# A count of TensorE's work that decides when products are issued and when their readers are written down, in a one-core Mamba and mixture-of-experts kernel

## The chip, the cores and the metric

The kernel runs on one core of a Trainium2 chip. The core has a matrix engine (TensorE, PE in the profile, with its weight loads as PEld), a vector engine (VectorE, DVE), an engine for activations and copies (ScalarE, ACT), GpSimd (POOL), which here multiplies and issues indirect DMAs, and SyncE (SP), which issues nearly all other DMAs. Each engine takes its instructions in the order in which the program wrote them. Matrix products land in PSUM, which has eight banks of 128 x 512 floats here. The metric is the time of one execution on the device in microseconds (us).

## The reference

A sequence of 4096 rows of width 256 goes through a Mamba block and a mixture of experts, each with a residual and a layer norm. Cut to what matters:

```python
# x: (1, 4096, 256) float32
xc, z = split(x @ W_in.T)                        # 512 + 512
u = silu(causal_conv(xc, taps of 4) + b_conv)
dt = softplus(u @ W_dt.T + b_dt);  Bm, Cm = u @ W_B.T, u @ W_C.T
# scan over time, 512 channels x 16 states
h = exp(dt * A) * h + dt * u * Bm;  y = sum_n(h * Cm)
x = layernorm(x + (y * silu(z)) @ W_out.T)

shared = (silu(x @ sg.T) * (x @ su.T)) @ sd.T
w = softmax(x @ router.T);  top = top_k(w + bias, 6);  w = w[top] / sum(w[top])
out = sum over the 6 experts of w_e * (silu(gate_e(x)) * up_e(x)) @ down_e + shared
x = layernorm(x + out)
```

There are 32 experts with 128 inner features; the shared expert has 256.

## The kernel before

**Tiling.** The 4096 rows go in NC = 8 chunks of 512. The scan is a chain of 512 units, 64 for each chunk: one unit is one state of 16 for one group of 128 channels over 512 steps of time. In a unit the scan (L1312) and the product with C (L1319) run on DVE, the exp (L1177) and the copy of the last state (`keep`, L1204) on ACT, dt*u*B (`du`, L1166) on POOL, and four transposes that add into y (L1223, `summed`, three units behind) on PE. The rows of B and C are broadcast to 128 partitions by DMA (`load_bc`, tiles bb and cb), three to four pairs of units ahead. There are six buffers of du, six of hc and three of h.

**Side work.** Everything else is written between the units by Python generators ("threads"). After each unit's instructions `step()` gives every living thread one turn, in the order in which they were appended; a thread writes a few instructions and yields. So a `yield` is a distance in the engines' program order, not a wait on the chip. `rounds(k)` is k yields; `beside(gens, gap)` starts generators `gap` turns apart and gives each a turn. The threads:

- `front(c+1)` (L889), during chunk c: loads and transposes x, projects it (px, L919), the convolution by taps as products (pv, L942), the gate of chunk c (`gate`, pz, L1039), silu (L961), B and C (pb, L969), then `stepped` (pd, L985, four products for the step sizes, with four ACT operations and two of DVE each), and the log part (L1015 to L1021). It ends with `load_x` four rounds later.
- `tail(c-1)` (L1068), during chunk c: reads the scan's result (pgt, L1080), the output projection (px, L1097), the layer norm, then `prepare` (L293): transposes, the router (pr, L323), top 6, `ranked` (pk, L438, and the places of each row in a sorted store xs), and after it the shared expert (`shared`: spg, spu, L370 and L384; spo, L402), whose result goes to acc by DMA.
- `copies(c)` (L563): 24 indirect DMAs on POOL that put the chunk's rows into xs, at most one a round, with a rest after every third.
- `load_rows(c)`: waits until the copies of chunk c-1 are written, then loads the rows for the tail.
- `tiles` (L733) and `pair` (L701): tiles of 128 sorted rows, two at a time. `loaded` issues the DMAs of the rows (xt), of the weights (gu, dn) on SP; `pair` transposes (pt, L668), multiplies (pg, L709), tanh and products (L717 to L721), the down projection (po, L727), and scatters into acc on POOL (L691). After a pair is begun, `tiles` rests four rounds. The tiles of a chunk are to be had once its copies are written, two chunks after its scan began.
- `walls`, `cleared`, `blanked`: DMAs alone. After the scan `through_all` (L1345) does the last two chunks' tiles with all weights held in SBUF, then `finish` does the last layer norm.

At the sixth unit before a chunk's end the front is drained: `drain` calls `step()` without writing units until the front has ended. `multiply` asserts at unit 33 of a chunk that the gate's silu is written.

**PSUM.** While the scan runs, side work has three banks. `room()` yields while all are held; `bank()` takes the next by rotation, whichever is free; `free()` counts down. A reader is written one or two rounds after its product:

```python
        def room():                       # L140
            while held[0] >= len(pools):
                yield
        def bank(name):                   # L144
            held[0] += 1
            turn[0] += 1
            return pools[turn[0] % len(pools)].tile([P, T], F32, tag="mm", name=name)
```

Of the kernel before, what the change touches and what calls it, by code (L numbers as in the profile page):

```python
# [60 lines left out]
def kernel(  # L61
# [70 lines left out]
    ps_m = ctx.enter_context(tc.tile_pool(name="ps_m", bufs=BANKS, space=PSUM))  # L132
# [3 lines left out]
    held, turn = [0], [0]  # L136

    pools = [ps_m] * BANKS

    def room():  # L140
        while held[0] >= len(pools):
            yield

    def bank(name):  # L144
        held[0] += 1
        turn[0] += 1
        return pools[turn[0] % len(pools)].tile([P, T], F32, tag="mm", name=name)

    def free():
        held[0] -= 1  # L150

# [11 lines left out]
    threads = []  # L163

    apart_from = [False]

    def step():
        threads[:] = [g for g in threads if alive(g)]
# [124 lines left out]
    def prepare(c):  # L293
# [9 lines left out]
        def turned(k):  # L303
            yield from room()
            pt = bank(f"pt_{c}_{k}")
            for b in range(nb):
                nc.tensor.transpose(pt[:, ts(b, P)], row[:, b, ts(k, P)], ident)
            yield
            nc.scalar.copy(x1T[:, k, :Tc], pt[:, :Tc])
            free()  # L310

        yield from beside([turned(k) for k in range(KD)], 1)
        nc.scalar.copy(
            row[:, :nb, ID : ID + 1],
            rows_f[:, AT[c] // P : AT[c] // P + nb].unsqueeze(2),
        )
        yield
        yield from room()
        pr = bank(f"pr_{c}")
        lg = pr[:, : nb * E].rearrange("p (b e) -> p b e", e=E)  # L320
        for b in range(nb):
            for k in range(KD):
                nc.tensor.matmul(  # L323
                    lg[:, b, :], x1T[:, k, ts(b, P)], rw[:, k, :],
                    start=(k == 0), stop=(k == KD - 1),
                )
        yield
        yield
        mx = stat.tile([P, NB], F32, tag="mx", name=f"mx_{c}")[:, :nb]
        nc.vector.tensor_reduce(mx, lg, AX.X, ALU.max)  # L330
        nc.vector.tensor_sub(prob, lg, mx.unsqueeze(2).to_broadcast([P, nb, E]))
        free()
        yield
        nc.scalar.activation(prob, prob, AF.Exp)
        yield
        sm = stat.tile([P, NB], F32, tag="sm", name=f"sm_{c}")[:, :nb]
        nc.vector.tensor_reduce(sm, prob, AX.X, ALU.add)
        nc.vector.reciprocal(sm, sm)
        nc.vector.tensor_mul(prob, prob, sm.unsqueeze(2).to_broadcast([P, nb, E]))


        score = stat.tile([P, NB, E + 2], F32, tag="score", name=f"score_{c}")[:, :nb]
        left = stat.tile([P, NB, E + 2], F32, tag="left", name=f"left_{c}")[:, :nb]
        top = stat.tile([P, NB, 8], F32, tag="top", name=f"top_{c}")[:, :nb]
        nc.vector.memset(score[:, :, E:], PAD)
        nc.vector.tensor_add(
            score[:, :, :E], prob, sbias.unsqueeze(1).to_broadcast([P, nb, E])
        )
        for b in range(nb):
            nc.vector.max(top[:, b, :], score[:, b, :E])  # L350
        nc.vector.memset(top[:, :, TOP_K:], PAD)
        yield
        for b in range(nb):
            nc.vector.match_replace(left[:, b, :], top[:, b, :], score[:, b, :], GONE)
        nc.vector.tensor_tensor(mask, left[:, :, :E], score[:, :, :E], ALU.not_equal)
        nc.vector.tensor_mul(prob, mask, prob)
        sm = stat.tile([P, NB], F32, tag="psm", name=f"psm_{c}")[:, :nb]
        nc.vector.tensor_reduce(sm, prob, AX.X, ALU.add)
        nc.vector.tensor_scalar(sm, sm, NORM_MIN, 2.0, ALU.max, ALU.mult)
        nc.vector.reciprocal(sm, sm)  # L360
        nc.vector.tensor_mul(
            row[:, :nb, WT:RW], prob, sm.unsqueeze(2).to_broadcast([P, nb, E])
        )
        yield from ranked(c, mask)

        def shared(i):
            yield from room()
            pg = bank(f"spg_{c}_{i}")
            for k in range(KD):
                nc.tensor.matmul(  # L370
                    pg[:, :Tc], sg_w[:, k, ts(i, P)], x1T[:, k, :Tc],
                    start=(k == 0), stop=(k == KD - 1),
                )
            yield
# [5 lines left out]
            free()  # L380
            yield from room()
            pu = bank(f"spu_{c}_{i}")
            for k in range(KD):
                nc.tensor.matmul(  # L384
                    pu[:, :Tc], su_w[:, k, ts(i, P)], x1T[:, k, :Tc],
                    start=(k == 0), stop=(k == KD - 1),
                )
            yield
            yield
            nc.vector.tensor_mul(hm, hm, pu[:, :Tc])  # L390
            free()
            hms.append(hm)

        for i in range(NSH):
            yield from shared(i)
        for h in range(nb // 2):
            yield
            yield from room()
            po = bank(f"spo_{c}_{h}").rearrange("p (b d) -> p b d", d=D)
            for b in range(2):  # L400
                for i in range(NSH):
                    nc.tensor.matmul(  # L402
                        po[:, b, :], hms[i][:, ts(2 * h + b, P)], sd_w[:, i, :],
                        start=(i == 0), stop=(i == NSH - 1),
                    )
            yield
            yield
            base = q1.tile([P, T], F32, tag="sg", name=f"base_{c}_{h}")
            base = base.rearrange("p (b d) -> p b d", d=D)
            nc.vector.tensor_add(base, po, row[:, 2 * h : 2 * h + 2, :D])  # L410
            free()
            yield from rounds(3)
            lo = AT[c] + 2 * h * P
            i = nc.sync.dma_start(
                acc[0][lo : lo + 2 * P, :].rearrange("(b p) d -> p b d", p=P), base
            )
            for j in adds:
                tc.declare_no_dep(i.ins, j, reason="rows of earlier chunks")

    def ranked(c, mask):  # L420
# [13 lines left out]
        yield from room()  # L434
        pk = bank(f"pk_{c}")
        flat = pk[:, : nb * E]
# [8 lines left out]
        yield  # L445
# [34 lines left out]
        free()  # L480
# [180 lines left out]
    def turned_rows(j, xt):  # L661
        yield from take("xsT", 2)
        yield from room()
        pt = bank(f"pt_{j}")
        pt4 = pt.rearrange("p (i k t) -> p i k t", i=2, k=KD)
# [3 lines left out]
        yield  # L669
        xT = q2.tile([P, 2, KD, P], F32, tag="xsT", name=f"xsT_{j}")  # L670
        nc.scalar.copy(xT.rearrange("p i k t -> p (i k t)"), pt)  # L671
        free()
# [6 lines left out]
    def added(j, po, wt, no, behind):  # L679
# [6 lines left out]
        free()  # L686
# [14 lines left out]
    def pair(j, xt, wt, gu, dn):  # L701

        xT, no = yield from turned_rows(j, xt)
        yield from room()
        pg = bank(f"pg_{j}").rearrange("p (h i t) -> p h i t", h=2, i=2)
        for h in range(2):
# [6 lines left out]
        give("xsT")  # L713
        yield from take("hm", 2)
        yield
# [6 lines left out]
        free()  # L722
        yield
        yield from room()
        po = bank(f"po_{j}").rearrange("p (i d) -> p i d", i=2)
        for i in range(2):
# [3 lines left out]
        yield  # L730
        yield from added(j, po, wt, no, False)

    def tiles(items):  # L733
# [4 lines left out]
        def begin(upto):  # L738
            while begun[0] < upto:
# [5 lines left out]
                yield from rounds(4 if items[k][2] else 3)  # L745
# [732 lines left out]
```

## Time and profile before

| what | value |
|---|---|
| median of three runs (range) | 1814.09 us (1813.79 to 1816.94) |
| the profiled execution | 1827.13 us, its span 1825.4 us |
| first scan starts, last ends | 61.1 us, 1559.5 us |
| chunks 0 to 7 of the scan | 145.7, 171.9, 184.9, 202.5, 205.1, 197.8, 195.5, 195.0 us |
| from the last scan to the first scatter of `through_all` | 39.5 us |
| mean granted clock of PE | 0.83 |

The chunks are read from the starts of every 64th scan in DVE's timeline. The first chunk has no tail and no pairs beside it, the second no pairs, the third eight pairs, chunks 3 to 7 some ten to twelve each; the last has no front. A position within a chunk ("unit 48") counts the scans written ahead of an instruction on DVE. Counted in this way the first chunk-wide steps of the tail stand at units 11 and 17 (L1105), the router's first reader at 26 (L330), the places at 32 or 33 (L484), the shared expert's readers at 43 to 59 (L379 to L410), the four pd readers at 29 to 39 (L997), and the last row of the log part at 46 to 48 (L1020).

In the lines of a profile, `idle before` is time in which the engine stood still ahead of that instruction, with what ended it. A wait's line has the total in us, how often, and the longest.

### The profile page before, as it was taken

How to read it: one execution, taken by the hardware profiler on the slowest of the kernel's cores; microseconds unless marked ns; L12 is line 12 of the kernel's file. 1: busy time of each engine (PE TensorE's matmuls, PEld its weight loads, DVE VectorE, ACT ScalarE, POOL GpSimd, SP SyncE). 2: the span in 40 equal slices, each digit the busy share in tenths (PEclk: the TensorE clock that was granted, in tenths of full speed). 3: DMA queues.
4: the chain of work that ended last, by engine and by line, in shares of the span. 5: the costliest groups of instructions: out<-in, count | busy, mean ns of one | idle time of the engine just before them, and what ended most of it. 6: DMA issues, size and time to landing. Idle time of an engine off the chain costs nothing. (4 is left out here: it accounts for less than half of the span.)

```text
span 1825.4 us, 23592 instructions
## 1 busy us (share of the span) xinstructions
PE 1310.7 (72%) x6068; PEld 916.8 (50%) x6068; DVE 1399.5 (77%) x2341; ACT 961.9 (53%) x2057; POOL 1184.6 (65%) x941
## 2 busy tenths in 40 slices
PE   7386696779675967699577977698677664885940
PEld 3243453456453634565465645565465543764730
DVE  4789979997998679868997789868998886441216
ACT  4567564547563656447554656457654532432533
POOL 0555544766587547776579548965797668466864
PEclk8597697679896988899788987899789787897975
DMA  9543782688577957797698858996699989975978
GB/s 254 152 119 105 231 290 78 161 228 239 134 177 204 251 146 171 213 248 193 127 246 216 242 133 193 248 245 176 151 249 274 274 192 264 231 120 112 145 105 344
DMA packets 307246, 359.62 MB, mean 197 GB/s; under 512 B 62368, under 2 KB 230048, under 8 KB 307104
## 3 DMA queue, kind: packets, MB, share of 16 engines
q1 hardware_dynamic: 266400, 302.82, 59.3%
q0 software_dynamic: 38592, 55.17, 16.9%
q8 instruction: 51, 0.84, 0.2%
q14 instruction: 91, 0.75, 0.1%
q10 hardware_dynamic: 2112, 0.05, 0.1%
HBM read 251.77 MB, written 106.15 MB: 196 GB/s over the span
## 5 line engine op out<-in xcount | busy, mean ns | idle before, releaser
L1166 POOL TENSOR_TENSOR du<-wall,bb 128x512 f32<-128x512 f32 x512 | 703.5, 1425 | 396.8 <-DVE h L1312 203.5
L1312 DVE TENSOR_TENSOR_SCAN h<-h,hlast,du 128x512 f32<-128x512 f32 x512 | 657.2, 1284 | 71.4 <-POOL du L1166 27.2
L1223 PE MATMUL y<-ident,hc 128*128 128x128 f32 x2048 | 340.2, 309 | 120.7 <-DVE hc L1319 105.4
L1177 ACT ACTIVATE h<-wall,aneg 128x512 f32<-128x512 f32 x512 | 354.0, 692 | 121.8 <-DVE hc L1319 96.6
L1319 DVE TENSOR_TENSOR hc<-h,cb 128x512 f32<-128x512 f32 x512 | 354.1, 692 | 55.4 <-DMA cb<-bcd 13.7
L1223 PEld LDWEIGHTS y<-ident,hc 128*128 128x128 f32 x2048 | 278.2, 161 | 217.6 <-DVE hc L1319 131.5
L691 POOL DMA_INDIRECT acc<-yt,no x136 | 215.5, 1584 | 93.2 <-ACT yt L685 44.8
L578 POOL DMA_INDIRECT xs<-row,at x192 | 191.7, 998 | 75.3 <-issue 33.7
L1204 ACT COPY hlast<-h 128x1 f32<-128x1 f32 x448 | 70.9, 158 | 252.2 <-DVE hc L1319 239.7
L727 PE MATMUL po<-dn,hm 128*128 128x256 f32 x272 | 96.5, 489 | 117.3 <-issue 58.1
L709 PE MATMUL pg<-xsT,gu 128*128 128x128 f32 x1088 | 147.6, 293 | 29.2 <-ACT xsT L671 25.4
L709 PEld LDWEIGHTS pg<-xsT,gu 128*128 128x128 f32 x1088 | 140.3, 206 | 46.3 <-ACT xsT L671 29.7
L691 POOL DMA_INDIRECT acc<-ytl,no x68 | 105.9, 1558 | 39.9 <-issue 20.1
L727 PEld LDWEIGHTS po<-dn,hm 128*128 128x128 f32 x272 | 60.1, 240 | 142.4 <-issue 68.5
L985 PE MATMUL pd<-wall 128*128 128x512 f32 x256 | 123.7, 631 | 10.2 <-ACT yt L685 5.9
L942 PE MATMUL pv<-wall 128*128 128x512 f32 x224 | 106.5, 619 | 7.4 <-ACT wall L924 3.8
L1362 DVE SCALAR_TENSOR_TENSOR gt<-gt,pg 128x256 f32<-128x256 f32 x34 | 14.3, 420 | 110.8 <-ACT gt L1360 68.3
L668 PE MATMUL pt<-ident,xt 128*128 128x128 f32 x408 | 71.9, 305 | 36.5 <-DMA xt<-xs 17.2
L668 PEld LDWEIGHTS pt<-ident,xt 128*128 128x128 f32 x408 | 56.8, 159 | 56.3 <-DMA xt<-xs 19.2
L985 PEld LDWEIGHTS pd<-wall 128*128 128x128 f32 x256 | 49.8, 204 | 65.0 <-issue 57.0
L720 DVE SCALAR_TENSOR_TENSOR gt<-gt,pg 128x256 f32<-128x256 f32 x68 | 28.1, 414 | 63.5 <-ACT gt L717 46.9
L671 ACT COPY xsT<-pt 128x512 f32<-128x512 f32 x102 | 59.5, 583 | 30.8 <-PE pt L668 22.7
(196 smaller groups left out, 1891.0 us busy)
## 6 DMA issues: line engine op xcount, KB each, us to landing
bb<-bcd SPq DMA_DIRECT2D x256, 256.0 KB
cb<-bcd SPq DMA_DIRECT2D x256, 256.0 KB
gu<-in_gate_up_t_dram SPq DMA_DIRECT2D x136, 256.0 KB
xs<-blank SPq DMA_DIRECT2D x55, 578.0 KB
xt<-xs SPq DMA_DIRECT2D x204, 128.5 KB
dn<-in_down_t_dram SPq DMA_DIRECT2D x136, 128.0 KB
wall<-acc SPq DMA_DIRECT2D x24, 512.0 KB
acc<-blank SPq DMA_DIRECT2D x16, 512.0 KB
```

The lines of the kernel that those rows point to most:

```text
L578: i = nc.gpsimd.indirect_dma_start(out=xs, out_offset=bass.IndirectOffsetOnAxis(ap=at[:, b, k : k + 1], axis=0), in_=row[:, b, :], in_offs ...
L668: nc.tensor.transpose(pt4[:, i, k, :], xt[:, i, ts(k, P)], ident)
L691: a = nc.gpsimd.indirect_dma_start(out=acc[(j + i) % LANES], out_offset=bass.IndirectOffsetOnAxis(ap=no[:, i : i + 1], axis=0), in_=yt[:, ...
L709: nc.tensor.matmul(pg[:, h, i, :], gu[i][:, k, ts(h, P)], xT[:, i, k, :], start=(k == 0), stop=(k == KD - 1),)
L727: nc.tensor.matmul(po[:, i, :], hm[:, i, :], dn[i], start=True, stop=True)
L942: nc.tensor.matmul(pv, taps[:, m, k, :], xin[:, m, k : k + Tc], start=(k == 0), stop=(k == TAPS - 1),)
L985: nc.tensor.matmul(pd, w_dt[:, k, ts(m, P)], u[:, k, :], start=(k == 0), stop=(k == M - 1),)
L1166: nc.gpsimd.tensor_mul(parts(q, du), u, row_for(q, 0))
L1177: nc.scalar.activation(h[:, ts(i, Tc)], dt_of[c][:, m + i, :], AF.Exp, scale=aneg[:, m + i, n : n + 1],)
L1223: nc.tensor.matmul(y_of[c, g][b // 2][:, b % 2, ts(m + j - 2 * g, P)], hc[:, ts(j * nb + b, P)], ident, start=(opens and j == 0 and b % 2 ...
L1312: nc.vector.tensor_tensor_scan(h, h, du_of.pop(q), hlast[:, n, m : m + 1], ALU.mult, ALU.add)
L1319: nc.vector.tensor_mul(parts(q, hc), parts(q, h), row_for(q, 1))
```

## The change

There are five parts.

1. A count of TensorE's work. `room(work)` gets a price for the product to be issued. `out_at` adds up the prices, `done_at` follows by PACE = 2.5 a round. While more than LITTLE = 2.3 is outstanding and the new product would bring it over 2.5, the thread yields. This holds while `paced` is set, from the first unit to the last.
2. Readers. `made()` takes the place of the yield between a product and its reader: one yield, and then more until the count has that product done. After the scan it is one yield.
3. Banks. A bank is taken from a list of free ones and goes back to it when its reader is written, each bank a pool of its own.
4. Order. `step()` sorts the threads: tail, tiles, pairs, front, others. The front's gap goes from 3 to 2. A pair may load once fewer than three have their gu products outstanding, and `tiles` rests one round after a pair of its own, not four.
5. In chunks but the last, routing and shared expert run beside each other, the second starting two rounds after the first.

```diff
+    PACE, LITTLE = 2.5, 2.3
+    out_at, done_at, paced = [0.0], [0.0], [False]
+
+    def room(work):
+        def full_up():
+            left = out_at[0] - done_at[0]
+            return held[0] >= len(pools) or (
+                paced[0] and left > LITTLE and left + work > PACE
+            )
+
+        while full_up():
+            yield
+        out_at[0] += work
+
+    def made(at=None):
+
+        at = out_at[0] if at is None else at
+        yield
+        while paced[0] and done_at[0] < at - 0.01:
             yield
 
     def bank(name):
         held[0] += 1
-        turn[0] += 1
-        return pools[turn[0] % len(pools)].tile([P, T], F32, tag="mm", name=name)
-
-    def free():
+        newest[0] = spare.pop(0)
+        return pools[newest[0]].tile([P, T], F32, tag=f"mm{newest[0]}", name=name)
+
+    def free(which):
         held[0] -= 1
+        spare.append(which)
...
+    FIRST = {"tail": 0, "tiles": 1, "pair": 2, "front": 3}
...
     def step():
+        done_at[0] = min(out_at[0], done_at[0] + PACE)
+
+        threads.sort(key=lambda g: FIRST.get(g.__name__, len(FIRST)))
         threads[:] = [g for g in threads if alive(g)]
...
+        if c < NC - 1:
+            yield from beside([routing(), sharing()], 2)
+        else:
+            yield from routing()
+            yield from sharing()
...
     def pair(j, xt, wt, gu, dn):
 
         xT, no = yield from turned_rows(j, xt)
-        yield from room()
+        yield from room(1.9)
         pg = bank(f"pg_{j}").rearrange("p (h i t) -> p h i t", h=2, i=2)
+        mine = newest[0]
...
         give("xsT")
+        give("gu")
+        at = out_at[0]
         yield from take("hm", 2)
-        yield
+        yield from made(at)
...
-                yield from rounds(4 if items[k][2] else 3)
+                yield from rounds(1 if items[k][2] else 3)
...
             if weights is not None:
+                yield from take("gu", 3)
                 yield from take("dn", 4)
...
-                yield from rounds(3 if c < NC - 1 else 2)
+                yield from made()
+                yield
                 part = row_of[c][:, 2 * h : 2 * h + 2, :D]
...
+        done_at[0], paced[0] = out_at[0], True
...
-                    mains.append(front(c + 1, 3))
+                    mains.append(front(c + 1, 2))
...
         scanned.append(True)
+        paced[0] = False
```

The other places go the same way: `room(w)`, the bank's number kept, `made()` for a yield, `free(mine)`. The prices:

| product | price | in a chunk |
|---|---|---|
| front: transposes of x, px, pv, pz, pb, pd | 0.8, 1.9, 3.6, 1.9, 3.6, 3.6 | 2, 4, 4, 4, 1, 4 |
| tail: pgt, px of L1097, transposes, pr, pk | 0.65, 3.6, 0.8, 1.4, 1.6 | 4, 2, 2, 1, 1 |
| tail: spg, spu, spo | 1.9, 1.9, 1.9 | 2, 2, 2 |
| pair: pt, pg, po | 0.65, 1.9, 1.0 | 12 each |

## The prediction

> **What bounds the kernel now.** I read the page's lines first, then the windows view of the scan, then the waits of VectorE (DVE), then windows inside a chunk.
>
> ```profile
> span 1825.4 us, 23592 instructions
> PE 1310.7 (72%) x6068; PEld 916.8 (50%) x6068; DVE 1399.5 (77%) x2341; ACT 961.9 (53%) x2057; POOL 1184.6 (65%) x941
> ...
> L1312 DVE TENSOR_TENSOR_SCAN h<-h,hlast,du 128x512 f32<-128x512 f32 x512 | 657.2, 1284 | 71.4 <-POOL du L1166 27.2
> ...
> L1319 DVE TENSOR_TENSOR hc<-h,cb 128x512 f32<-128x512 f32 x512 | 354.1, 692 | 55.4 <-DMA cb<-bcd 13.7
> ```
>
> Each of the 512 units costs DVE 1.284 + 0.692 us. The first scan starts at 61.1 us, the last ends at 1559.5; the next window is that whole stretch. Columns are length, then busy time (and instructions) of PE, PEld, DVE, ACT, POOL, then granted clock, DMA share, GB/s.
>
> ```profile
> 61.10:1559.50 1498.40, 1114.38 (x5170) 772.09 (x5170) 1288.12 (x2005) 823.96 (x1738) 1011.41 (x807) 0.83 0.76 200
> ```
>
> DVE is busy 1288 of 1498 us, so 210 us are idle and 86% is work that this change leaves as it is. The waits of DVE in that stretch:
>
> ```profile
> DVE gt L720 <- ACT gt L717: 43.3, 10, 7.1
> DVE h L1312 <- POOL du L1166: 27.2, 23, 2.3
> DVE h L1312 <- ACT h L1177: 26.4, 18, 3.5
> DVE h L1312 <- ACT hlast L1204: 16.2, 8, 3.9
> DVE hc L1319 <- DMA cb<-bcd: 13.7, 6, 3.9
> ```
>
> 43 + 26 + 16 us end at ScalarE (ACT), and ACT's own timeline tells why. At 1024.3 us it had waited 5.44 us for the convolution's product, with the tanh and the scan's exp queued behind:
>
> ```profile
> 1018.19 0.69 ACT L1177 ACTIVATE h<-wall,aneg 128x512 f32<-128x512 f32 x1
> 1024.32 0.69 ACT L947 ACTIVATE wall<-pv,bcv 128x512 f32<-128x512 f32 x1 [5.44 <-PE pv L942]
> 1026.10 0.38 ACT L717 ACTIVATE gt<-pg 128x256 f32<-128x256 f32 x1 [1.10 <-PE pg L709]
> ```
>
> So a reader written one round after its product stops ACT, then DVE, then GpSimd (POOL). Is TensorE (PE) then the bound? Units 6 to 25 of chunks 3, 4, 5 and 6, in windows:
>
> ```profile
> 576.50:639.00 62.50, 57.27 (x273) 39.78 (x273) 43.12 (x58) 34.91 (x79) 35.30 (x28) 0.95 0.89 245
> 787.00:844.50 57.50, 55.70 (x260) 37.13 (x258) 44.73 (x57) 34.22 (x75) 38.52 (x30) 0.96 0.91 246
> 986.50:1048.60 62.10, 60.41 (x279) 40.61 (x280) 43.74 (x59) 36.74 (x80) 41.16 (x31) 0.92 0.92 241
> 1184.30:1249.60 65.30, 60.44 (x307) 42.44 (x306) 46.22 (x59) 41.48 (x87) 41.47 (x33) 0.97 0.88 233
> ```
>
> Yes, there: PE is busy 234 of 247 us near full clock and DVE 178. From unit 25 on DVE is the bound again (71.5 of 76 us from 1093 to 1169, with PE at 53).
>
> **The change, part by part.** The sum is made against the profiled execution (span 1825.4, whole run 1827.1), which lies 0.7% above the median 1814.09; the difference in us is then taken off the median. DVE, ACT, PE and POOL keep every instruction; the edits move them in their queues, and add no wait of an engine but by the new order.
>
> *Pace, late readers, free banks, priorities.* The prices in the new calls are about what PE takes at full clock (px is 4 matmuls, 1.72 us, priced 1.9). Per chunk the front is priced 49.2, the tail 25.8, and 12 pairs at 3.55 make 42.6: 117.6, or 47 rounds at 2.5, of 64. The y transposes are not counted; two units of them take 1.04 us. So a full round gives PE 2.5 + 0.52 = 3.02 us.
> (a) Units 6 to 25 are then at most 19 x 3.02 = 57.4 us of PE. Full throughout, the four stretches save 5.1 + 0.1 + 4.7 + 7.9 = 17.8 us; with PE never in the way they shrink to DVE's work and save 247.4 - 177.8 = 69.6. Tail, front and pairs all ask for the pace there, so I take -27, near the full case.
> (b) In units 25 to 34 of the same chunks (639.0 to 687.6, 844.5 to 891.0, 1048.6 to 1092.6, 1249.6 to 1289.2; 178.7 us) DVE is busy 151.0. The idle 27.7 stands mostly before gt and h. Late readers can take it all or, if PE is still behind, nothing: -14. The bank rotation is in here: PE waited at L668 19.3 us for other things than its rows (36.5 idle, 17.2 of it for xt), one part being banks still to be read.
> (c) In units 0 to 6 of chunks 4 to 6, 51.4 us against DVE's 41.3, POOL (47.7) is late with scatters of pairs that ran over the edge. Pairs now come every 2.5 to 4 rounds, not 5.5, and are over by then, but copies end later (next part): 0 to -10, I take -4.
>
> *Routing beside the shared expert.* Its DVE work (6 instructions of 0.68, 4.1 us a chunk) and its two DMAs to acc move some 15 units forward. That costs DVE nothing, but it takes banks while the routing waits for one; with three banks, each now held until the counted end, I put the routing some 6 rounds later. The 24 copies take 32 rounds and now end about unit 8 of the next chunk, not 1; load_rows, the tail and the pairs wait for them. The scan covers this, except at the end (e).
>
> *The front last in line.* Before, its last multiplication (L1020) stands at unit 47 or 48 and load_x at 52; at unit 58 the front is drained without scans. The gaps of 2 save 6 rounds, the counted waits add about as many, and standing last costs more. One bound: the assertion in multiply wants the gate's silu by unit 32; it was at 23, so 9 late at most, and load_x at 61.
> (d) The price of drained rounds is read where the first front runs with no scans (43.9 to 52.6): DVE idles 2.01 us before each row of pd and about 1.1 us in each two rows of Ln. Four pd and two Ln pairs: 10.2 us a chunk, five chunks (2 to 6), 51; none: 0. I take 3 a chunk, +15; DVE's scans of units 55 to 57, still queued, hide the rest.
>
> *The end.* (e) Four own pairs were left after the scan; their PE work, some 3.3 us each, stands in the chain from 1563 to 1587. Gone: -13. But if the copies of chunk 6 run 11 beyond the scan, at 1.28 us on POOL, the last rows load later: +14. I take -4, since the later scatters (68 x 1.86 us on POOL, 1.56 and 0.30 before it) stay.
>
> *Pairs closer together.* (f) Twelve pairs load 12 x 1.025 MB (two each of 128.5, 256 and 128 KB), and SP's queue, which also carries bb and cb, gets them closer together. DMA share is already 0.88 to 0.92 in units 6 to 25 and about 0.55 in 25 to 34. A pair with its two scatters of 128 KB, read and written, moves by estimate 1.55 MB, 6.2 us at 250 GB/s. Chunk 5's DMA work is 0.80 x 198 = 158 us, so the rest is (158 - 74)/198 = 0.42 us per us. Spread over 38 units (at 3 us, 114) that is 48 + 74 = 122, so 8 over, mostly hidden by loads three pairs ahead. In the loader's own 2.5 rounds (90 us): 112, so 22 over. 0 to +75 (15 x 5 chunks); I take +5.
>
> Chunks 0 to 2 and 7 otherwise at nothing (bound: chunks 1 and 2 could give 15; 7 waits for POOL and DMA).
> Sum: -27 - 14 - 4 + 15 - 4 + 5 = -29. 1814 - 29 = **1785 us**.
>
> **Rivals.**
> *B, the stalls really go.* (a) at 60 (most of 69.6), (b) at 25, (c) 8, the rest as above: -60 - 25 - 8 + 12 = -81, 1733. For it: pace and prices fit PE's rows. Against: in runs of plain units (2.0 us on DVE) PE gets 2.0 us where the count credits 3.02.
> *C, slower: the transfers become the bound.* Place: units 8 to 40 of chunks 3 to 7. PE stands at pt or pg for rows and weights, with y queued behind, so DVE runs out of hc buffers. Price 15 us a chunk: -29 - 5 + 75 = +41, 1855. It decides from (75 - 41)/5 = 6.8 us a chunk, a spacing below some 38 units per twelve pairs. For it: DMA share 1.00 from 987 to 1008 us, POOL's 103.9 us of waits for bb. Against: banks and the pace hold pairs back.
> *D, slower: the front is drained at full price*: -29 - 15 + 51 = +7, 1821. For it: the front is last, and PE is asked 47 of 58 rounds. Against: the assertion's bound.
> *E, slower: a thinner stream loses PE's clock.* It is 1.00 from 1008 to 1032, where PE never rests, 0.79 from 1093 to 1169, and 0.50 after 1765, where it does nothing. If units 6 to 25 fell from 0.95 to 0.79, 57.4 us would be 69.0: 4 x 11.6 = +46, 1831. The Trainium skill (TensorE: Matmul & The Clock Gate, Part 1) says the clock halves after an idle window of some 3.4 us, and full rate needs one busy; by that rule, gaps of a round would cost this, and the rows named agree in direction. Against: a full round leaves PE no gap.
> *N, it does not do what it says*: the count runs in rounds, not us, so readers are as early as before where rounds are short; 1812 or so.
>
> **From these to numbers.** Forecast 0.40, B 0.24, C 0.17, D 0.09, E 0.04, N 0.06. Faster is forecast and B, 0.64; within 0.2% (what a measurement here can tell from no change) N, 0.06; slower C, D, E, 0.30. The forecast's own range is 1765 to 1805. To hold eight in ten it goes from B's middle to just under C: 1728 to 1850.
>
> **What would show it.** (a) right: units 6 to 25 take 53 to 57 us with PE near full. (b): DVE gt L720 <- ACT gt L717 below 20 us, ACT wall L947 <- PE pv L942 (100.3) below 40. (d): L1020 last at unit 55 or later and gaps near unit 58 of chunks 3 to 6. (e): no pairs of L727 after the last scan. C: PE pt or pg waiting for DMA by tens of us, DMA share 1.0 past unit 25. E: clock below 0.9 in units 6 to 25. I am wrong if DVE's idle in the scan stays at 200 us or more, or falls below 140.

## The result and the profile after

| | before | after |
|---|---|---|
| median of 7 runs each, us | 1812.26 | 1801.11 |
| ratio, 95% interval | | 0.9936, 0.9916 to 0.9956 |
| profiled span, us | 1825.4 | 1799.4 |
| scan, first to last unit, us | 1498.4 | 1483.2 |
| idle time of DVE in it, us | 210.3 | 193.8 |
| after the scan, us | 265.8 | 255.2 |

The changed kernel is faster by 0.64%, 11 us, where 29 us were forecast. The profiled execution of before lies some 14 us above its own median of the same chip (a second one, on another chip, has a span of 1816.2), so the 26 us between the two spans are more than the medians show.

From the page of after, totals and groups:

```profile
span 1799.4 us, 23620 instructions
PE 1276.7 (71%) x6068; PEld 905.9 (50%) x6068; DVE 1398.3 (78%) x2341; ACT 959.1 (53%) x2057; POOL 1184.1 (66%) x941
...
L1371 DVE TENSOR_TENSOR_SCAN h<-h,hlast,du 128x512 f32<-128x512 f32 x512 | 657.1, 1283 | 60.3 <-POOL du L1223 35.6
...
L1378 DVE TENSOR_TENSOR hc<-h,cb 128x512 f32<-128x512 f32 x512 | 354.3, 692 | 54.0 <-DMA cb<-bcd 11.5
...
L725 ACT ACTIVATE yt<-po,wt 128x256 f32<-128x256 f32 x136 | 56.5, 466 | 107.1 <-DMA acc<-yt,no 82.0
```

The same work of ACT before, from the list of its lines:

```profile
L685 ACT ACTIVATE yt<-po,wt 128x256 f32<-128x256 f32 x136 | 56.2, 464 | 10.9 <-DMA wall<-in_down_t_dram 3.5 <-PE po L727 3.1 <-DMA acc<-yt,no 2.6
```

PE and DVE have as many instructions as before, and DVE is as long busy (1398.3 us against 1399.5), so in the scan a stretch is shorter where DVE idles less. The wait of the scaling of a pair's result (`yt`) is new: before, it waited 2.6 us for its DMA (`acc`), now 82. L1371 is the scan (L1312 before), L725 the writing of `yt`, L731 its two scatters.

The windows view of after has the same columns as in the prediction. First units 6 to 25 of chunk 5 and the sum over chunks 3 to 6; then units 0 to 6 of chunks 4, 5 and 6; then the whole of chunk 7:

```profile
961.40:1010.90 49.50, 48.35 (x225) 32.33 (x226) 42.07 (x57) 31.24 (x71) 35.70 (x28) 0.96 1.00 270
...
sum 201.50, PE 195.25 PEld 130.51 DVE 168.84 ACT 126.44 POOL 141.86; mean PE 48.81 PEld 32.63 DVE 42.21 ACT 31.61 POOL 35.47
...
740.90:765.80 24.90, 14.87 (x84) 12.07 (x84) 15.12 (x21) 10.18 (x28) 21.16 (x18) 0.77 0.91 235
936.10:961.40 25.30, 15.59 (x84) 12.87 (x84) 15.10 (x22) 9.73 (x27) 23.16 (x19) 0.77 0.93 243
1131.50:1157.30 25.80, 15.02 (x84) 12.31 (x84) 15.03 (x21) 9.30 (x26) 22.94 (x19) 0.78 0.90 237
1324.80:1544.30 219.50, 133.10 (x726) 110.48 (x725) 164.72 (x262) 81.28 (x158) 157.60 (x123) 0.80 0.89 242
```

The same stretches of before:

```profile
971.30:986.50 15.20, 10.44 (x55) 8.27 (x53) 13.52 (x18) 6.87 (x18) 14.17 (x13) 0.84 0.80 211
1169.00:1184.30 15.30, 11.11 (x54) 7.99 (x53) 13.48 (x18) 6.74 (x17) 14.13 (x12) 0.74 0.98 270
1364.50:1559.50 195.00, 122.52 (x667) 100.39 (x666) 157.52 (x255) 77.57 (x146) 144.66 (x114) 0.81 0.94 246
```

PE's stretch went from 247.4 to 201.5 us, more than forecast. But PE's work in it fell from 233.8 to 195.3 us as well: part of the "gain" is work that now stands elsewhere. The first six units of chunks 5 and 6 take 25 us in place of 15, with POOL busy for 23 of them, and chunk 7 takes 24.5 us more. Added up by the starts of the units (the last column is the experiment routing_then_sharing, below; the first row is a whole of three chunks, the next five are chunks 3 to 6):

| stretch, us | before | after | after, routing first |
|---|---|---|---|
| chunks 0 to 2 | 503 | 489 | 491 |
| units 0 to 6 | 64 | 95 | 58 |
| 6 to 25 | 247 | 202 | 227 |
| 25 to 40 | 239 | 210 | 204 |
| 40 to 48 | 88 | 91 | 93 |
| 48 to 64 | 162 | 178 | 176 |
| sum of chunks 3 to 6 | 801 | 775 | 758 |
| chunk 7 | 195 | 220 | 192 |
| after the scan | 266 | 255 | 265 |

A second profile of the changed kernel (after_again, below) has the same pattern: 91, 208, 211, 91 and 182 us in the five stretches, 223 in chunk 7 and 259 after the scan.

What happens at the edge is seen in the timelines of chunk 5's first units: POOL, ACT and DVE of after, with the idle time ahead of an instruction in brackets:

```profile
949.64 1.61 POOL L731 DMA_INDIRECT acc<-yt,no  x1 [0.17 <-ACT hlast L1261]
950.70 1.85 POOL L1223 TENSOR_TENSOR du<-wall,bb 128x512 f32<-128x512 f32 x1
...
959.36 0.84 ACT L725 ACTIVATE yt<-po,wt 128x256 f32<-128x256 f32 x2 [7.65 <-DMA acc<-yt,no]
960.08 0.38 ACT L760 ACTIVATE gt<-pg 128x256 f32<-128x256 f32 x1
...
960.50 0.42 DVE L763 SCALAR_TENSOR_TENSOR gt<-gt,pg 128x256 f32<-128x256 f32 x1 [7.31 <-ACT hlast L1261]
```

`yt` has two buffers. A pair's result can be written only when the scatters of an earlier pair have read theirs, and a scatter stands in POOL's queue between the `du` of the scan, then takes some microseconds to land. ACT stands for 7.65 us, with the next pair's tanh queued behind, and DVE, with the scan behind that pair's product, for 7.31. By the position of DVE's instructions the pairs of chunk 5 stand at units 1, 2, 5, 16, 22, 29, 35, 41, 49, 54, 57 and 61; before at 3, 7, 16, 21, 27, 32, 38, 44, 52, 55 and 61. In the middle of the chunk the pairs are held back a little (units 22, 29, 35 and 41 in place of 21, 27, 32 and 38); they come close together when the tail and the shared expert are through, across the edge, where the last of the 24 copies (L617) are still in POOL's queue, as they were before. What lets them come so close is also the rest of one round in place of four between pairs: rest_of_four, below, gives the four back, and the wait for acc is nearly gone.

ACT's waits in the scan, the first line before the change, the others after:

```profile
ACT wall L947 <- PE pv L942: 100.3, 27, 8.1
...
ACT yt L725 <- DMA acc<-yt,no: 78.7, 17, 11.0
...
ACT gt L760 <- PE pg L750: 49.9, 27, 8.1
...
ACT wall L1040 <- PE pd L1035: 14.6, 9, 3.3
...
ACT wall L995 <- PE pv L990: 12.2, 4, 4.9
```

The convolution's wait (L995, L947 before) went from 100.3 to 12.2 us, as the late readers were meant to do, and the one for pd from 48.1 to 14.6; the one for pg grew from 23.6 to 49.9. Together these three fell from 172 us to 77, and the new wait of `yt` gives 79 of it back.

### The profile page after: what moved, and what is told of

Same layout as the page of the kernel before. It is cut to its first block, busy times and chain, and to the rows that moved or that the text cites. A ratio compares the mean times of both kernels' runs of the same rounds, so it can differ in the third digit from the quotient of the medians.

```text
span 1799.4 us, 23620 instructions
## 1 busy us (share of the span) xinstructions
PE 1276.7 (71%) x6068; PEld 905.9 (50%) x6068; DVE 1398.3 (78%) x2341; ACT 959.1 (53%) x2057; POOL 1184.1 (66%) x941
## 5 line engine op out<-in xcount | busy, mean ns | idle before, releaser
L1223 POOL TENSOR_TENSOR du<-wall,bb 128x512 f32<-128x512 f32 x512 | 678.8, 1373 | 376.8 <-DVE h L1371 191.7
L1371 DVE TENSOR_TENSOR_SCAN h<-h,hlast,du 128x512 f32<-128x512 f32 x512 | 657.1, 1283 | 60.3 <-POOL du L1223 35.6
L1378 DVE TENSOR_TENSOR hc<-h,cb 128x512 f32<-128x512 f32 x512 | 354.3, 692 | 54.0 <-DMA cb<-bcd 11.5
L731 POOL DMA_INDIRECT acc<-yt,no x136 | 216.8, 1594 | 60.5 <-issue 15.9
L617 POOL DMA_INDIRECT xs<-row,at x192 | 190.6, 993 | 87.3 <-issue 38.4
L731 POOL DMA_INDIRECT acc<-ytl,no x68 | 106.4, 1565 | 54.3 <-ACT hT L1435 29.6
L1035 PE MATMUL pd<-wall 128*128 128x512 f32 x256 | 120.0, 615 | 16.6 <-DVE shm L420 11.2
L771 PE MATMUL po<-dn,hm 128*128 128x256 f32 x272 | 85.0, 443 | 61.7 <-issue 18.1
L725 ACT ACTIVATE yt<-po,wt 128x256 f32<-128x256 f32 x136 | 56.5, 466 | 107.1 <-DMA acc<-yt,no 82.0
L1424 DVE SCALAR_TENSOR_TENSOR gt<-gt,pg 128x256 f32<-128x256 f32 x34 | 14.3, 421 | 113.1 <-ACT gt L1422 113.1
L771 PEld LDWEIGHTS po<-dn,hm 128*128 128x128 f32 x272 | 54.2, 220 | 77.2 <-issue 25.2
```

The lines of the kernel that those rows point to most:

```text
L617: i = nc.gpsimd.indirect_dma_start(out=xs, out_offset=bass.IndirectOffsetOnAxis(ap=at[:, b, k : k + 1], axis=0), in_=row[:, b, :], in_offs ...
L731: a = nc.gpsimd.indirect_dma_start(out=acc[(j + i) % LANES], out_offset=bass.IndirectOffsetOnAxis(ap=no[:, i : i + 1], axis=0), in_=yt[:, ...
L771: nc.tensor.matmul(po[:, i, :], hm[:, i, :], dn[i], start=True, stop=True)
L1035: nc.tensor.matmul(pd, w_dt[:, k, ts(m, P)], u[:, k, :], start=(k == 0), stop=(k == M - 1),)
L1223: nc.gpsimd.tensor_mul(parts(q, du), u, row_for(q, 0))
L1371: nc.vector.tensor_tensor_scan(h, h, du_of.pop(q), hlast[:, n, m : m + 1], ALU.mult, ALU.add)
```

## The experiments

The ratios are to the kernel before on the same chip, with a 95% interval; its median there was 1821 to 1824 us.

**before_again**: the kernel before once more.

> The kernel before, unchanged, for a second profile: its profiled execution (1827.1 us) lay some 15 us above the median of its runs. If that profile was a usual one, the chunks come out within 2 us each as before (202.5, 205.1, 197.8, 195.5, 195.0 for 3 to 7). If it was an odd one, the span is about 1811 us and the difference stands in a few places, which are then not to be counted as gains of the change.

One run of 1817.9 us, span 1816.2; chunks 0 to 7 take 145.4, 171.9, 184.3, 201.0, 203.4, 198.3, 194.5 and 192.7 us, within 3 us of the first profile each. The stretches of the table differ by at most 4 us between these two profiles, and by at most 7 between the two of the changed kernel. So the table's differences of 15 us and more are the change's. DVE's idle time in the whole scan (202.0 us here) differs by 8 and 14 us between profiles of one kernel, which is as much as between the kernels.

**yt_third_buffer**

```diff
-    yt = (...).tile([P, 2, D], F32, tag=tag, name=f"{tag}_{j}", bufs=n)
+    yt = (...).tile([P, 2, D], F32, tag=tag, name=f"{tag}_{j}", bufs=n if behind else 3)
```

> The changed kernel with a third buffer of yt, still at most two taken. Theory S (the pairs now come in bursts and ACT stands before yt until an earlier scatter has read its buffer): ACT's idle time before yt that ends with DMA acc falls from 82 us to under 25, DVE's waits that end with ACT (gt and h, 66 us) to under 45, and the time by 12 to 25 us. Rival P (at those places POOL itself is the bound, with scatters, copies and du): the wait at yt goes, but du takes its place, units 0 to 6 of chunks 4 to 6 stay at 24 to 26 us, and the time moves by less than 5 us.

0.9835 (0.9809 to 0.9862), as theory S had it. ACT's wait for acc falls to 6.2 us and units 0 to 6 of chunks 4 to 6 fall from 25 us to 18 or 20. But part of it goes to other waits of DVE:

```profile
DVE h L1371 <- POOL du L1223: 52.2, 39, 5.2
DVE hc L1378 <- DMA cb<-bcd: 33.9, 12, 6.8
```

They were 35.6 and 11.5 us. One reading, which this run does not prove: the burst loads several queues at once, and the wait shows at whichever gives way first.

**rest_of_four**: pairs kept apart.

```diff
-                yield from rounds(1 if items[k][2] else 3)
+                yield from rounds(4 if items[k][2] else 3)
```

> The changed kernel with four rounds of rest after a pair, as before. Theory S: the bursts at the chunk's edge (readers of pairs at units 54, 57, 61, 1, 2, 5) are drawn apart, ACT's waits at yt fall below 40 us, and the time falls by 5 to 15 us. Rival Q (the pairs are held back by banks and the pace, and what waited comes out at once whatever the rest): positions stay within two units, the time within 4 us; more pairs left after the scan would cost up to 10.

0.9830 (0.9795 to 0.9866), somewhat more than theory S had. Chunk 5's pairs now stand at units 5, 12, 20, 25, 32, 40, 48, 52, 57 and 60; the wait for acc falls to 4.7 us, DVE idles 151 us, and the scan ends at 1509.6 us. Nine of the 68 pairs are left for after the scan, which takes 278.8 us.

**no_pace**

```diff
-        done_at[0], paced[0] = out_at[0], True
+        done_at[0], paced[0] = out_at[0], False
```

> The changed kernel with the count switched off, so that products go out when a bank is free and readers are written one round later; everything else as changed. If the pace gave the gain in units 6 to 25: they go back from about 50 us to 58 or more in each of chunks 3 to 6, ACT's waits at pv, pd and pg from about 60 us to over 150, and the time is 15 to 40 us above the changed kernel, so not below the kernel before. Rival (free banks, order and the earlier shared expert gave it): within 8 us of the changed kernel.

1.0505 (1.0474 to 1.0537). ACT waits 118 us in `yt` for acc, 67 for pv, 58 for pd, 52 for pg and 46 for pt. The other parts without the count are far worse than the kernel before. Two things go with this switch: `made()` too stops counting, so the late readers are left out as well as the pace. And the wait for acc stands here without any count, so it is not the count alone that brings it.

**after_again**, **both_mended**, **early_readers** and **late_give**. The first is the changed kernel; the second has a third buffer for yt and the rest of four.

> The changed kernel as it is, beside the others of this call. Both theories: 0.990 to 0.996 of the kernel before, ACT waiting some 80 us in yt for acc, DVE idle some 190 us in the scan.

0.9931 (0.9915 to 0.9948), the same as in the result.

> The changed kernel with a third buffer for yt and a rest of four rounds between pairs. Theory S (the bursts of pairs fill yt's two buffers and ACT stands): each mend alone took the wait away, so together they add little: 0.980 to 0.985, no more than 6 us below the better of the two. Rival P (what is left after either mend is GpSimd running late with the scatters of the burst, so the mends work on different waits): the gains add, 0.970 to 0.977, with h<-POOL du below 35 us and DVE idle below 150.

0.9815 (0.9797 to 0.9833): the mends add next to nothing to each other, so they act on one thing. DVE idles 153 us in the scan.

The next edit is that of early_readers.

```diff
-        while paced[0] and done_at[0] < at - 0.01:
+        while False:
             yield
```

> The changed kernel with the starts of products still paced, but each reader written one round after its product, as before the change. Theory R (the late readers are what took ACT's waits for TensorE away): ACT's waits for pv, pd and pg come back, 100 us or more together, and units 6 to 25 of chunks 3 to 6 take 230 us or more; ratio 0.998 to 1.01. Rival T (the paced starts alone do it, since never more than a round's work stands ahead of a product): those waits stay below 60 us together, units 6 to 25 below 215, ratio 0.985 to 0.996.

1.0142 (1.0115 to 1.0169): the late readers are worth 2 points, more than either theory said. ACT's waits with early readers:

```profile
ACT gt L760 <- PE pg L750: 78.0, 40, 3.9
ACT wall L1040 <- PE pd L1035: 66.6, 25, 4.1
ACT wall L995 <- PE pv L990: 50.0, 19, 8.4
```

195 us together, against 77 in the changed kernel and 172 before. The count alone doesn't take them away. The next edit is that of late_give.

```diff
             adds.append(a.ins)
+        if not behind:
+            yield from rounds(4)
         give(tag)
```

> The changed kernel with two buffers for yt, but a buffer is counted free only four rounds after its second scatter is written, not at once. Theory S: ACT's wait in yt for acc falls from 82 to below 20 us, since a pair now waits in its thread and not on ACT; ratio 0.980 to 0.988. Rival P: the pairs held back take banks and the pace from the others, so the time goes elsewhere; the ratio stays 0.990 or more.

1.0011 (0.9994 to 1.0029), a miss for theory S. The wait for acc fell from 82 to 30 us, and units 0 to 6 of chunks 3 to 6 from 95 to 70, but units 6 to 25 went from 202 to 223 and units 25 to 40 from 210 to 219: the pairs wait in their threads, still two buffers at a time, and come just as close (units 1, 2, 5 and 56, 57, 61, 62 in chunk 4). DVE waits 38 us for cb and 44 for du. So to take away the one wait in which the burst showed is not enough; that the burst itself costs fits this run and the mends above.

**rest_in_last_chunk**: the rest of four in chunk 7 alone (`now[0]` holds the chunk).

```diff
-                yield from rounds(1 if items[k][2] else 3)
+                yield from rounds((4 if now[0] == NC - 1 else 1) if items[k][2] else 3)
```

> The changed kernel with the rest of four rounds between pairs in chunk 7 alone. Theory S (the burst is what costs, wherever it stands): some 4 pairs go back behind the scan, chunk 7 falls from 219.5 to about 200 us, the end grows by 11 to 15, net 5 to 9 us: ratio 0.988 to 0.991; units 0 to 6 of chunks 4 to 6 stay at 24 to 26 us each. Rival E7 (chunk 7 is long because it has fifteen pairs of work in it, not because they come in bursts): what the chunk gains the end loses, 0.992 to 0.996.

0.9857 (0.9823 to 0.9891). Chunk 7 takes 197.6 us, three pairs go behind the scan, and the end is 264.3. So fifteen pairs in chunk 7 at a rest of one round cost more than twelve there and three after it; the gain is larger than in either expectation.

**order_of_arrival**: the sort in `step()` left out.

> The changed kernel with the threads stepped in the order in which they were begun, as before the change, instead of tail, tiles, pairs, front. Theory A (the prediction's: the order lets the front come last and costs drained rounds; undone, pairs come later): L1020's successor moves ahead of unit 50, pairs fall back, more than 2 pairs after the scan; ratio 0.990 to 1.000. Rival O (the order matters to nothing but who comes first, since the pace binds all): 0.991 to 0.996, pairs per chunk as in the changed kernel within 1.

1.0027 (1.0007 to 1.0047), outside both expectations, and the front's last row stays at units 53 and 54. Twelve pairs are left after the scan, which ends earlier (at 1529.0 us), and the end takes 295.6 us, in place of 255 to 259. The order is worth a point, above all by bringing pairs forward.

**banks_in_turn** and **banks_in_turn_2**

```diff
-    ps_m = ctx.enter_context(tc.tile_pool(name="ps_m", bufs=1, space=PSUM))
+    ps_m = ctx.enter_context(tc.tile_pool(name="ps_m", bufs=BANKS, space=PSUM))
...
-        return pools[newest[0]].tile([P, T], F32, tag=f"mm{newest[0]}", name=name)
+        return pools[newest[0]].tile([P, T], F32, tag="mm", name=name)
```

> The changed kernel with its banks taken in turn again, out of one pool, instead of a free one. Theory F (the counted readers come out of the order of the products, so a bank in turn is often still to be read): TensorE waits for readers of other banks, units 6 to 25 of chunks 3 to 6 go from 202 to 215 us or more, ratio 1.000 to 1.015. Rival G (no more than three products stand at once and each is read within two rounds, so the order of banks hardly differs): 0.991 to 0.996.

> Banks in turn out of one pool during the scan, and in turn out of all eight after it, as before the change; the first such kernel had only one bank more after the scan in place of five. Theory G (the order of the banks hardly differs): 0.991 to 0.996. Rival F: 1.000 or more.

The first took 1.0277 (1.0233 to 1.0322), all of it after the scan: its scan is as long as the changed kernel's (1483.0 us), and the end, with one bank more where five are meant, takes 325.8. With that mended, 0.9901 (0.9869 to 0.9932): no gain from taking free banks can be told. The first run is a warning: its ratio alone would have spoken for theory F, which the second does not bear out.

**routing_then_sharing**: the fifth part undone.

```diff
-        if c < NC - 1:
+        if False:
             yield from beside([routing(), sharing()], 2)
```

> The changed kernel with the shared expert after the routing, as before the change. Theory A (the prediction's: side by side holds the routing back some 6 rounds): the routing's last step moves from unit 33 to 27 or so and the ratio is 0.990 to 0.994. Rival Q (side by side costs the routing nothing and only brings the shared expert forward): the routing stays at 31 to 33, the shared expert's last sum goes from unit 47 to 55 or later, the front ends later and is drained or collides with the pairs: 0.996 to 1.006.

0.9702 (0.9676 to 0.9728), outside both expectations: without this part the change gives 3%. The routing's last step stays at unit 32 or 33, as rival Q had it; the shared expert's last sum goes to units 58 to 61. Units 0 to 6 of chunk 5, and chunk 7:

```profile
928.60:943.00 14.40, 11.92 (x69) 9.68 (x69) 14.05 (x20) 9.57 (x25) 12.44 (x11) 0.88 0.92 243
1310.00:1501.70 191.70, 128.51 (x687) 107.58 (x687) 163.99 (x259) 80.28 (x153) 144.11 (x113) 0.80 0.93 253
```

The edge is without stalls (DVE 14.05 of 14.40), and ACT's wait for acc is 21 us. The pairs hardly move for that: in chunk 5 they stand at units 3, 4, 9, 18, 23, 29, 33, 37, 48, 56, 59 and 63, so eight of them come before unit 48 here as in the changed kernel.

**sequence_third_buffer**, **sharing_later** (`beside([...], 14)` in place of 2) and **shared_quarter** ask why.

> Routing first and then the shared expert, with a third buffer for yt. Theory S2 (side by side costs because the shared expert's products push the pairs out of units 25 to 48 and together at the chunk's edge, where yt's buffers run out; in sequence the pairs are far enough apart): the third buffer adds at most 0.4%, 0.966 to 0.972. Rival I (the buffers and the sequence are two costs of their own): it adds the 1% that it gave to the changed kernel, 0.958 to 0.964.

0.9700 (0.9657 to 0.9744): in sequence no gain of the buffer can be told, so its gain and that of the sequence are not two.

> Side by side, but the shared expert begins 14 rounds after the routing, not 2. Theory S2 (what matters is where the shared expert's work stands): its last sum moves from unit 47 to 55 or later, out of the stretch where PE is full, and most of the gain of the sequence comes: 0.970 to 0.980. Rival H (two generators taking banks and the pace from each other cost by themselves): 0.985 to 0.995.

0.9781 (0.9745 to 0.9817): the later place alone brings two thirds of it. It does so although units 56 to 64 of chunks 4 and 5 take 27 and 34 us in this run, against 21 in the changed kernel; the front's last row stands at unit 57 there.

> The changed kernel with a quarter of the matmuls of the shared expert's gate and up products in chunks 0 to 6 (the three others of each four left out), prices as they were, so each instruction keeps its round. Theory S2 (the shared expert costs through the rounds that it takes from the pairs, not through PE's time itself): TensorE has 5.2 us a chunk less to do and the ratio still stays at 0.986 or more. Rival T2 (PE's time in units 25 to 48 is what makes the chunk longer): the chunks lose 4 us or more each, ratio 0.970 to 0.980.

0.9939 (0.9912 to 0.9966), as the changed kernel. These products have two steps in k each, so this kernel leaves out half of them, and not three quarters as the expectation says. The rows of gate and up fall from 62.8 to 33.5 us over the scan, 4.2 us a chunk, and chunks 4 to 6 still take 195, 198 and 196 us. So this much of TensorE's time isn't what makes the chunks longer; what stays the same in this run are the rounds that the products take.

**pairs_first** and **sequence_rest_two**

```diff
-    FIRST = {"tail": 0, "tiles": 1, "pair": 2, "front": 3}
+    FIRST = {"tiles": 0, "pair": 1, "tail": 2, "front": 3}
```

> The changed kernel, side by side as it is, but tiles and pairs are stepped ahead of the tail. Theory S2 (the shared expert costs by the rounds that it takes from pairs of lower rank): the pairs are no longer held back in units 25 to 48, the bursts at the edge get thinner, ACT's wait in yt for acc falls below 40 us, ratio 0.972 to 0.985. Rival V (the routing, now behind the pairs too, gives its rows out later, and the pairs of the next chunk start later and burst just the same): 0.988 or more.

1.0315 (1.0297 to 1.0333), on the side of rival V: the tail comes late (from chunk 3 on its routing ends at units 35 to 45), the front behind it too, and in chunks 2 and 5 units 56 to 64 take 36.1 and 33.6 us, against some 20.

> Routing first and then the shared expert, with a rest of two rounds between pairs. Theory S2 (in sequence the pairs hardly burst any more): little is left to gain, 0.967 to 0.973. Rival W (the three pairs of units 2 to 9 still cost): 0.960 to 0.966.

0.9903 (0.9886 to 0.9919): a rest of two rounds in place of one loses two points, a miss for both theories. DVE's timeline in chunk 5, at the unit from which the front is run to its end without scans (L442 is the shared expert's sum, L763 a pair's product):

```profile
1098.50 0.69 DVE L1378 TENSOR_TENSOR hc<-h,cb 128x512 f32<-128x512 f32 x1
...
1106.67 0.42 DVE L763 SCALAR_TENSOR_TENSOR gt<-gt,pg 128x256 f32<-128x256 f32 x1 [4.11 <-ACT gt L760]
...
1111.32 0.69 DVE L442 TENSOR_TENSOR base<-spo,row 128x512 f32<-128x512 f32 x1 [2.43 <-PE spo L434]
...
1115.17 1.28 DVE L1371 TENSOR_TENSOR_SCAN h<-h,hlast,du 128x512 f32<-128x512 f32 x1
```

For nearly 17 us DVE runs no scan: the other way in which a schedule that is a little later pays. Units 56 to 64 take 34.6 us there. Chunk 7, with bursts again (two pairs at unit 2, then 53, 57, 59 and 61), takes 212.1.

## Why the prediction was right and wrong

The sign was right, and so was the mechanism of (a) and (b): ACT's stalls before products of TensorE are what the change removes. The size was not. The steps that failed are (c), "Pairs now come every 2.5 to 4 rounds, not 5.5, and are over by then", chunk 7 "at nothing", and the routing beside the shared expert, which "costs DVE nothing". The runs show a burst of pairs at the chunks' edges (24.5 us where (c) had -4), a chunk 7 that is 24.5 us longer, and a fifth part without which the change gives 3.0% in place of 0.7%.

DVE's idle time by stretch is the better account, since work that moves to another stretch hardly changes it. In units 6 to 25 it fell by 37 us (from 70 to 33), in units 25 to 40 by 19, and in chunks 0 to 2, which the sum had at nothing, by 12. It grew by 26 in units 0 to 6, by 7 in units 48 to 64 and by 17 in chunk 7. In the second profiles of both kernels the falls are 24, 18 and 8, the growth 23, 10 and 22. So (a) and (b), 41 us in the sum, came out at 56 and 42, and most of what the scan gained (in the second profiles all of it) was lost again elsewhere in it.

- **(a)** -27; the profile shows -46 in units 6 to 25. PE is full there (195.3 of 201.5 us), as the step had it. But a unit gives PE 2.57 us, not the 3.02 that the step allowed, so more work than forecast leaves this stretch, and nothing in the sum let it land anywhere.
- **(b)** -14 up to unit 34; units 25 to 40 give -29, again partly work that goes on to units 40 to 48, where PE is now busy 22.3 of 22.7 us. The step's own sign came by name (`gt` behind ACT's `gt`, 18.6 us, below 20), but the same instruction now waits 23.6 us that end with `hlast`, another of ACT: 42.2 us together, after 50.7.
- **(c)** -4; the first six units of chunks 4 to 6 went up by 24.5 us, and units 48 to 64 of chunks 3 to 6, which the sum left out, by 16. What is held back in the middle comes in a burst at the edge. Drawn apart, or with a third buffer, it is worth a point (rest_of_four, yt_third_buffer).
- **(d)** +15; it did not come. L1020's successor stands last at unit 55, as said, but units 56 to 64 of chunks 3 to 6 take 82 us in all, as before. The price is real, though, and higher than the 10.2 us of the step's bound: where the front is drained (sequence_rest_two, pairs_first), units 56 to 64 take 13 to 18 us more.
- **(e)** -4; the four pairs are gone and the end is 10.7 us shorter, near the bound of -13 (5.4 between the second profiles of both kernels). The pairs landed in chunk 7, which is 24.5 us longer. The step saw what the end gives up, not who takes it.
- **(f)** +5, no sign of more: DVE's wait for cb went from 13.7 to 11.5 us. PE's wait for xt grew to 34.3 us at pt, with no wait of DVE behind it in that size.
- **The routing beside the shared expert** was costed at nothing for DVE, at six rounds for the routing and at later copies. The routing and the copies are where they were, and the part costs 2.3 points. Why is not fully shown. The tail ranks ahead of the pairs, so shared-expert rounds moved to units 25 to 47 may be rounds taken from pairs; sequence_third_buffer, sharing_later and shared_quarter came out as this theory had it. Against it, as many pairs as in the sequence stand before unit 48, the two at 35 and 41 only two and four units later, and pairs_first, made to test it, missed. With a rest of two rounds the sequence gives only 1%. How much of the 2.3 points is the place of this work and how much that this one schedule happens to fit, stays open.

In the sums, (d), (e) and (f) as above make +16 in rival B, not +12, so 1737 and not 1733; nothing hangs on it.

Of the rivals, B's size did not come. Of C one sign came in part, PE's 34.3 us at pt, but not the slower kernel, and the DMA share is 0.52 to 0.54 in units 25 to 40 and at most 0.90 in units 40 to 64. D's price is real, but its front was done in time. E did not come either: the granted clock in units 6 to 25 is 0.95 to 0.97, and over the scan 0.85 where it was 0.83. At the edge it is 0.77, where PE is busy 60% and in chunk 5 stands still for 6 us at a stretch. The Trainium skill's rule (TensorE: Matmul & The Clock Gate, Part 1), by which the clock falls after an idle window, agrees with this in direction. N's time was nearly met (1801 against 1812), but not its mechanism: the readers are later, as the wait for pv shows. As for the idle time of DVE, 193.8 us, it lies just inside the bounds that the prediction set for itself (140 to 200); in after_again, on another chip, it is 207.7 and outside.

The value of the parts, from the runs that leave one out (the changed kernel 0.9931): the count with the late readers that hang on it 5.7 points, the late readers by themselves 2.1, the order 1.0, the rest of one round in place of four -1.0, free banks nothing that can be told, routing beside the shared expert -2.3. The front's gap and the limit on gu were not undone by themselves. The best kernel of all runs is the changed one with routing first, 1768.6 us against 1822.2; a third buffer for yt makes no difference to it that can be told.

## What to carry to other kernels

A limit on how fast work is handed out saves time only if what it holds back has a place to go: list where each postponed instruction lands, and look there for buffers that are sized for the old spacing. A sum by stretches that credits a shorter stretch must subtract the work that left it; the idle time of the engine that is the bound needs no such correction. Undo each part of a change by itself, and try a neighbouring setting: here one part cost more than the whole gain, and one round more of rest cost two points (sequence_rest_two).

## What was unexpected of the hardware

A scatter keeps its source buffer busy long after POOL has issued it. POOL is busy 1.6 us with the issue; for the 35 of the 136 scatters of `yt` whose landing the trace shows, it comes a median of 5.8 us after the issue began, and 4.2 us after POOL was done with it. Two of them stand near chunk 5's edge, with 4.2 and 7.9 us. ACT, which writes that buffer next, waited up to 11.0 us. The Trainium skill (DMA: Bandwidth & Descriptors, Anatomy of one DMA — SWDGE (gpsimd) path) gives a DMA from this engine about 2 us plus its bytes over 436 GB/s, by estimate 2.3 us for 128 KB. The accumulating scatters of this kernel, with the DMA engines 0.75 busy over the scan, take longer than that, and the measurement decides.

Half of the shared expert's gate and up products, 4.2 us of TensorE a chunk, could be left out without a difference in time that can be told (0.9939 against 0.9931). They stand in units 25 to 35, where PE is busy 71%, and not in units 6 to 25, where it is busy 97%.
